# A state-space block with a binarised MLP on one core: scan tiles laid out in interleaved pairs, the norm's inverse root as a power on POOL, buffers in thirds

## The chip, the core and the metric

One of the cores of a Trainium2 chip runs the whole kernel. The metric is the device time in microseconds (us) of one execution; three executions of the kernel before took 3263.69, 3261.21 and 3260.56 us, median 3261.21.

The engines are called as the profile calls them: PE (TensorE, matmuls), PEld (its weight loads), DVE (VectorE), ACT (ScalarE), POOL (GpSimd) and SP (SyncE, which here only issues DMAs).

## The reference, cut to what matters

The input x is 8 images of 384 channels and 32 x 32 places; all data are float32. B = 8, C = 384, L = 1024.

```python
# norm over channels, twice (eps 1e-6, then 1e-5)
t = layernorm(ln_c(x)) * ln_w + ln_b                    # (b, L, 384)
xm, z = split(t @ in_proj_w.T)                          # 768 each
xc = silu(causal_conv_3_taps(xm) + conv_b)
dt, Bm, Cm = split(xc @ x_proj_w.T, [24, 40])           # 24, 16, 16
dt = softplus(dt @ dt_proj_w.T + dt_proj_b)             # (b, L, 768)
dA  = exp(dt[..., None] * A)                            # (b, L, 768, 16)
dBu = (dt * xc)[..., None] * Bm[:, :, None, :]
h_t = dA_t * h_(t-1) + dBu_t                            # scan over L
y = sum_n(h * Cm) + xc * D
t = (y * silu(z)) @ out_proj_w.T
x = x + gelu(t @ mlp_w1.T + mlp_b1) @ mlp_w2.T + mlp_b2
# the second layer, of which only the first 5 images get a part other than zero
q = quantise(ln_t(x) @ sign(W1 - mean).T + b1)          # per image: clip(a * 128 / (max|a| + eps))
x = x + quantise(gelu(q) @ sign(W2 - mean).T + b2)
```

The rows of W1 and W2 fall into 5 groups, each with a mean of its own.

## The kernel before, in words

The kernel is written as a list of operations which a planner in it, `Plan` (lines 163 to 349), puts into an order. Each `add` names an engine, a budget in us, the tiles it reads and writes, and a function that issues the instructions. `Plan.run` (line 221) goes through a simulated time: it takes the engine that can start first, chooses by lane and image (`rank`, line 256), issues the operation, and reckons its end from the budget. A DMA's end is reckoned at lines 332 to 334: 1.0 us after its issue, then its bytes at 395e3 per us on one shared line, then 0.9 us. The engines run what the planner issued in that fixed order, each its own queue. Where PE would be idle for over 0.7 us in the plan, lines 311 to 321 issue short matmuls without use, the tile `spare`. Buffers are rings of a fixed number (line 369), and a piece of work starts only when its ring has a free buffer.

For each image b, in halves of T = 512 places:

- `s1` (line 598), the front. `norm` (line 543) sums over channels with column-strip matmuls (`columns`, p_sum and p_var), spreads the mean over the partitions with a matmul (`spread`, p_mean), subtracts, squares, takes Sqrt on ACT and the reciprocal on DVE (lines 585 to 590), and spreads that (p_r). Then p_in and the convolution, Silu in place on the whole 128 x 3072 tile `xc`, p_dbc (dt's 24 rows, B and C), p_bc (line 698, which adds the two halves of B and C), six matmuls p_dt (line 722), Softplus, dt * xc on POOL (line 732), and the gate p_z with Silu. The results go to DRAM: xc, z, dt and dtx as whole tiles of 1.5 MB, B and C as rows.
- `s2` and `scan` (lines 748 and 761), the scan. A unit m holds four groups of 32 channels. For images 1 to 6 a tile is 128 x 1024: 32 channels times four of the 16 states, over all places. Images 0 and 7 are scanned in two halves with a tile of two groups by 512 places and a kept `state`. `rep` loads dt and dtx with every row repeated four times, `quad_rows` a row of B or C for each state. `scan_tile` (line 870) makes, for each tile: da = exp(dt * A) on ACT, into PSUM; u = dtx * B on POOL (line 886); the scan on DVE (line 890); the product with C on POOL (line 904) or on DVE (line 907), as `on_pool` (line 866) says. Then py (line 842) sums over the states with matmuls of 32 columns, four of which fill the array, and `zr` takes y * silu(z) to DRAM. Both inputs of POOL's products lie in SBUF; DVE's da lies in PSUM.
- `s3` (line 912): out_proj (p_out), the MLP's first matmuls (p_h), Gelu on two tiles of 128 x 3072, and the second ones (p_o, `mlp_out`, line 977).
- `ffn` (line 1092) for images 0 to 4: norm, p_y from the binarised W1, the maximum, then y1 again from DRAM in tiles of 1.5 MB, clip on POOL, Gelu, p_y from W2, the maximum, clip, addition. `binarise` (line 988) runs once: it sums W by matmuls with ones (p_sums, line 1018), takes the means and the signs.

The matmuls of most stages have line 494, ACT's functions line 510, and copies with a scale and a bias 523 to 532 (`affine`, which the planner may give to ACT, DVE or POOL).

Of the kernel before, what the change touches and what calls it, by code (L numbers as in the profile page):

```python
# [26 lines left out]
F32 = mybir.dt.float32  # L27
# [15 lines left out]
HK = KH // 2  # L43
T = 512
# [49 lines left out]

def c_pool(n):
    return 0.18 + n * 0.00214
# [33 lines left out]
class Piece:  # L130
# [8 lines left out]

    def __getitem__(self, part):  # L140
        return self, part

# [13 lines left out]
class Op:  # L156
    __slots__ = (
        "engine", "cost", "emit", "prio", "slack", "table", "size",
        "wants", "next", "ready", "tiles", "others", "settle",
# [3 lines left out]
class Plan:  # L163
# [12 lines left out]
    def add(self, engine, cost, emit, r=(), w=(), claim=(), table=None, size=0, others=None):  # L176
# [3 lines left out]
        op.size, op.prio = size, (*self.prio, len(self.ops))  # L180
# [40 lines left out]
    def run(self):  # L221
# [60 lines left out]
        while left:  # L282
# [49 lines left out]
            if e == "SP":  # L332
                dma_free = max(dma_free, end + 1.0) + op.size / 395e3
                end = dma_free + 0.9
# [17 lines left out]
class Layer:  # L352
    def __init__(self, ctx, tc, a, out):
# [9 lines left out]
        def ring(tag, bufs, where=sbuf):  # L363
# [7 lines left out]
            "front": ring("front", 2), "t_f": ring("t_f", 2), "w_f": ring("w_f", 3),  # L371
            "dbc": ring("dbc", 1), "halo": ring("halo", 2),

            "dt_r": ring("dt_r", 3), "dtx_r": ring("dtx_r", 3), "u": ring("u", 9),
# [4 lines left out]
            "yg": ring("yg", 1), "hid": ring("hid", 2), "t_b": ring("t_b", 1), "w_b": ring("w_b", 3),  # L379
            "w6": ring("w6", 2), "w6_n": ring("w6_n", 2), "res": ring("res", 2),  # L380

            "t_n": ring("t_n", 2), "small": ring("small", 7),

            "mm": ring("mm", 3, psum), "sq": ring("sq", 1),
            "rstd": ring("rstd", 2),
# [6 lines left out]
        for b in range(B):  # L392
            for name in ("dt", "dtx"):
                self.dram[name, b] = handed(f"{name}_d{b}", [DI, L])
# [24 lines left out]

    def constants(self):
        nc, a, const = self.nc, self.a, self.const
        small = const.tile([P, 3], F32, name="small")
        one, self.eps_m, self.eps_f = (small[:, i : i + 1] for i in range(3))
        for at, value in ((one, 1.0), (self.eps_m, E1 * E2), (self.eps_f, E_FFN)):
            nc.vector.memset(at, value)
# [8 lines left out]
        self.pick = const.tile([P, 2 * NS], F32, name="pick")  # L436
        nc.vector.tensor_add(self.pick, ident[:, DQ : 2 * DQ], ident[:, DP + DQ : DP + 2 * DQ])
        self.edge = const.tile([P, KD, 2], F32, name="edge")
# [23 lines left out]
    def load(self, to, view, src, r=(), size=0, cost=0.4):  # L462

        self.plan.add(
            "SP", cost, lambda: self.nc.sync.dma_start(view(to.real), src), r=r, w=[to],
            size=size,
        )

    def store(self, dst, frm, view, w, size, cost=0.4):
# [802 lines left out]
```

## Time and profile before

| | before |
|---|---|
| median of three executions | 3261.21 us |
| the profiled execution, and its span | 3262.23 us, 3260.4 us |
| mean granted clock of PE | 0.984 |
| DMA traffic | 748.73 MB in 367345 packets, 230 GB/s |

PE's busy time holds the pipelined matmuls with their modelled ends; each float32 matmul stands as two records, so that x1152 is 576 matmuls. A group's line gives: source line, engine, operation, output and inputs, shapes, count, busy us, mean ns of one record, and the idle time of that engine just before it with what ended it. The costliest that the change leaves alone are:

```profile
L494 PE MATMUL p_h<-t,w_b 128*128 128x512 f32 x1152 | 513.6, 600 | 10.9 <-DMA w_b<-in_mlp_w 9.9
L494 PE MATMUL p_o<-g,w 128*128 128x512 f32 x1152 | 506.7, 595 | 5.4 <-ACT g L510 2.9
L890 DVE TENSOR_TENSOR_SCAN da<-da,u 128x1024 f32<-128x1024 f32 (+1 forms) x416 | 840.5, 2020 | 111.6 <-POOL u L886 62.9
L890 DVE TENSOR_TENSOR_SCAN u<-da,u 128x1024 f32<-128x1024 f32 (+1 forms) x352 | 699.5, 2010 | 90.3 <-ACT da L510 63.0
```

The transfers that the change touches, with KB each and the median us from issue to landing:

```profile
dtx_r<-dtx_d SPq DMA_DIRECT2D x144, 512.0 KB, 5.8
dt_r<-dt_d SPq DMA_DIRECT2D x144, 512.0 KB, 6.0
w_b<-in_mlp_w SPq DMA_DIRECT2D x192, 192.0 KB, 2.9
...
w_f<-in_in_proj_w SPq DMA_DIRECT2D x168, 192.0 KB, 4.2
...
gf<-y_d SPq DMA_DIRECT2D x20, 1536.0 KB, 9.5
```

### The profile page before, as it was taken

To read this page: it belongs to the slowest core of one execution; us is meant where nothing else is said; L and a number is where in the kernel's file an instruction comes from. 1 tells how busy PE (TensorE), PEld (TensorE's weight loads), DVE (VectorE), ACT (ScalarE), POOL (GpSimd) and SP (SyncE) were. 2 spreads that over 40 slices of the span, in tenths; PEclk is the share of its full clock that TensorE was granted. 3 is DMA by queue.
4 is the path that set the end of the run, shared out by engine and by line. 5 is a ranking of instruction groups with operands and counts; after the bars stand their busy time and mean duration, and the time that the engine had idled before them with its cause. 6 is when DMAs were issued, how large, how long until landed. Compare 5 with 4: busy or idle time off the path is not lost.

```text
span 3260.4 us, 34027 instructions
## 1 busy us (share of the span) xinstructions
PE 3122.5 (96%) x11098; PEld 1317.7 (40%) x11098; DVE 2742.3 (84%) x2127; ACT 2024.3 (62%) x2246; POOL 2848.7 (87%) x1371
## 2 busy tenths in 40 slices
PE   8988999999999999999899999999999999999999
PEld 4333433444433434334334344343443534433334
DVE  4778899799978899888998878999788988789880
ACT  4778787656665576665656566755666565656551
POOL 1688899979999989999989999989999899999970
PEclk9998999999999999999999999999999999999999
DMA  6988778657796568675686667866677656766542
GB/s 218 305 282 276 249 250 294 221 183 234 259 322 197 184 230 291 229 238 197 208 298 211 237 211 246 295 225 226 220 275 250 207 185 205 249 187 207 167 141 76
DMA packets 367345, 748.73 MB, mean 230 GB/s; under 512 B 33856, under 2 KB 111168, under 8 KB 367168
## 3 DMA queue, kind: packets, MB, share of 16 engines
q1 hardware_dynamic: 366736, 746.46, 68.5%
q8 instruction: 89, 1.46, 0.2%
q14 instruction: 88, 0.72, 0.1%
q10 hardware_dynamic: 432, 0.09, 0.0%
HBM read 566.06 MB, written 180.36 MB: 229 GB/s over the span
## 4 chain that ended last, share of the span: by engine, by line
PE 74%; DMA 9%; DVE 6%; ACT 5%; issue 2%; POOL 2%; SPq 1%; ACTq 0%; DVEq 0%; POOLq 0%
PE p_y L494 17%; PE p_o L494 14%; PE p_h L494 13%; PE py L842 9%; PE p_out L494 6%; PE p_z L494 6%; PE p_in L494 5%; DVE da L890 2%; DMA w<-in_out_proj_w 2%; DMA w_f<-in_in_proj_w 2%; DVE u L890 1%; ACT L510 1%; DMA w_b<-in_mlp_w 1%; ACT da L510 1%; PE spare L412 1%
## 5 line engine op out<-in xcount | busy, mean ns | idle before, releaser
L886 POOL TENSOR_TENSOR u<-dtx_r,bc 128x1024 f32<-128x1024 f32 x768 | 1790.4, 2362 | 72.3 <-DMA dtx_r<-dtx_d 46.3
L510 ACT ACTIVATE da<-dt_r,a_neg 128x1024 f32<-128x1024 f32 (+1 forms) x960 | 902.7, 945 | 534.0 <-DVE u L907 331.1
L904 POOL TENSOR_TENSOR u<-u,bc 128x1024 f32<-128x1024 f32 x352 | 828.4, 2364 | 121.5 <-DVE u L890 115.5
L890 DVE TENSOR_TENSOR_SCAN da<-da,u 128x1024 f32<-128x1024 f32 (+1 forms) x416 | 840.5, 2020 | 111.6 <-POOL u L886 62.9
L890 DVE TENSOR_TENSOR_SCAN u<-da,u 128x1024 f32<-128x1024 f32 (+1 forms) x352 | 699.5, 2010 | 90.3 <-ACT da L510 63.0
L494 PE MATMUL p_h<-t,w_b 128*128 128x512 f32 x1152 | 513.6, 600 | 10.9 <-DMA w_b<-in_mlp_w 9.9
L907 DVE TENSOR_TENSOR u<-da,bc 128x1024 f32<-128x1024 f32 x416 | 507.9, 1221 | 10.5 <-ACT state L901 0.3
L494 PE MATMUL p_o<-g,w 128*128 128x512 f32 x1152 | 506.7, 595 | 5.4 <-ACT g L510 2.9
L842 PE MATMUL py<-u,fold 128*32 128x512 f32 x3072 | 376.6, 605 | 4.5 <-DVE u L907 4.5
L494 PEld LDWEIGHTS p_h<-t,w_b 128*128 128x128 f32 x1152 | 214.7, 190 | 298.1 <-issue 256.4
L494 PEld LDWEIGHTS p_o<-g,w 128*128 128x128 f32 x1152 | 215.9, 190 | 292.0 <-issue 277.3
L494 PE MATMUL p_y<-tn,w_b 128*128 128x512 f32 x720 | 324.9, 598 | 4.0 <-DVE tn L592 3.3
L494 PE MATMUL p_y<-gf,w_n 128*128 128x512 f32 x720 | 319.0, 599 | 6.7 <-DMA w_n<-bin_w 4.0
L510 ACT ACT_TABLE_LOAD x222 | 284.8, 1283 | 11.7 <-DVE xc L661 7.3
L494 PE MATMUL p_out<-yg,w 128*128 128x512 f32 x552 | 249.2, 604 | 8.9 <-DMA w<-in_out_proj_w 4.3
L494 PE MATMUL p_z<-t,w_f 128*128 128x512 f32 x504 | 232.5, 611 | 8.2 <-DMA w_f<-in_in_proj_w 6.2
L494 PE MATMUL p_in<-t,w_f 128*128 128x512 f32 x504 | 228.3, 602 | 10.8 <-DMA w_f<-in_in_proj_w 8.6
L494 PEld LDWEIGHTS p_y<-gf,w_n 128*128 128x128 f32 x720 | 135.1, 191 | 187.6 <-issue 172.4
L494 PEld LDWEIGHTS p_y<-tn,w_b 128*128 128x128 f32 x720 | 133.9, 190 | 183.9 <-issue 155.4
L842 PEld LDWEIGHTS py<-u,fold 128*32 128x32 f32 x3072 | 81.5, 110 | 261.1 <-issue 203.2
L525 ACT ACTIVATE g<-p_h,v_vecs 128x512 f32<-128x512 f32 x157 | 106.3, 681 | 120.9 <-PE p_h L494 120.7
L525 ACT ACTIVATE y<-p_y,v_vecs 128x512 f32<-128x512 f32 x138 | 94.1, 683 | 130.0 <-PE p_y L494 100.3
(112 smaller groups left out, 2700.3 us busy)
## 6 DMA issues: line engine op xcount, KB each, us to landing
dtx_r<-dtx_d SPq DMA_DIRECT2D x144, 512.0 KB, 5.8
dt_r<-dt_d SPq DMA_DIRECT2D x144, 512.0 KB, 6.0
w_b<-in_mlp_w SPq DMA_DIRECT2D x192, 192.0 KB, 2.9
w<-in_mlp_w SPq DMA_DIRECT2D x96, 384.0 KB, 3.6
w_f<-in_in_proj_w SPq DMA_DIRECT2D x168, 192.0 KB, 4.2
y_d<-y SPq DMA_DIRECT2D x120, 256.0 KB, 3.4
gf<-y_d SPq DMA_DIRECT2D x20, 1536.0 KB, 9.5
xc_d<-xc SPq DMA_DIRECT2D x16, 1536.0 KB, 7.3
```

Source lines behind the costliest of these rows:

```text
L412: self.plan.fill = lambda: self.nc.tensor.matmul(self.plan.spare.real[:, : 2 * P], self.ones, self.one.to_broadcast([P, 2 * P]), start=Tru ...
L494: self.nc.tensor.matmul(p.real, w.real[:, w0 + k, :], t.real[:, k0 + k, :], start=start and k == 0, stop=stop and k == n - 1,)
L510: lambda: self.nc.scalar.activation(out(), in_(), func, **{k: v() if callable(v) else v for k, v in kw.items()}),
L525: nc.scalar.activation(out(), in_(), AF.Identity, bias=bias, scale=scale)
L842: nc.tensor.matmul(py.real[p0 : p0 + DQ, :], self.fold, hc, start=False, stop=(q == NQUAD - 1), skip_group_check=True,)
L886: add("POOL", 2.36, lambda: nc.gpsimd.tensor_mul(u.real, dtx_r.real, spread(bq)), r=[dtx_r, bq], w=[u])
L890: add("DVE", (0.2 if half else 0.15) + n * 0.00209, lambda k=k, col=col: nc.vector.tensor_tensor_scan(to.real[:, k, :], da.real[:, k, :], ...
L904: add("POOL", 2.36, lambda: nc.gpsimd.tensor_mul(u.real, u.real, spread(cq)), r=[cq], w=[u])
L907: add("DVE", 1.21, lambda: nc.vector.tensor_mul(u.real, da.real, spread(cq)), r=[da, cq], w=[u])
```

## The change

1. **Interleaved pairs.** Two scan tiles lie in one buffer u of [128, wide, n, 2], the second tile's elements between those of the first. POOL multiplies both in one instruction, with B or C repeated for each pair. DVE's scan and product and the py matmuls read and write the pair's halves with a stride of two elements. The last quarter of the states writes into the dtx buffer itself. Channels are regrouped on the host to suit. `on_pool` gives POOL the C product of 9 in 16 tiles (before 11 in 24).
2. **Norm.** p_var is scaled and copied, turned by a matmul with columns of the identity (p_turned), and eps is added on DVE; POOL raises [128, 4] to the power -0.5. The Sqrt and the reciprocal go.
3. **Front.** p_bc becomes p_all, one matmul that adds the halves of B and C and copies dt's rows twice, to partitions 0 and 32; p_dt then runs in pairs on two strips of 32 rows. dt * xc writes interleaved.
4. **Thirds.** xc, z, dt, yg, the MLP's g and gf are tiles of [128, 2, 512], with the activations, the stores and loads on them in thirds or sixths. yg, z of image 1 and the MLP's pieces share one ring of nine; p_o runs in six parts of two matmuls.
5. **Binarise.** p_sums uses 32-column strips of the array; the groups are summed on DVE, and a small matmul (p_means) adds the lanes.
6. **Planner.** A transfer's end is reckoned with a landing time by kind, and budgets of issues are changed.

```diff
@@ planner, rings
+def c_pair(n):
+    return 0.19 + n * 0.00188
...
             if e == "SP":
-                dma_free = max(dma_free, end + 1.0) + op.size / 395e3
-                end = dma_free + 0.9
+                dma_free = max(dma_free, end + 0.5) + 0.05 + op.size / 360e3
+                end = dma_free + op.land
...
-            "front": ring("front", 2), "t_f": ring("t_f", 2), "w_f": ring("w_f", 3),
+            "front": ring("front", 7), "t_f": ring("t_f", 2), "w_f": ring("w_f", 3),
...
-            "dt_r": ring("dt_r", 3), "dtx_r": ring("dtx_r", 3), "u": ring("u", 9),
+            "dt_r": ring("dt_r", 3), "dtx_r": ring("dtx_r", 2), "u": ring("u", 3),
...
-            "yg": ring("yg", 1), "hid": ring("hid", 2), "t_b": ring("t_b", 1), "w_b": ring("w_b", 3),
-            "w6": ring("w6", 2), "w6_n": ring("w6_n", 2), "res": ring("res", 2),
-
-            "t_n": ring("t_n", 2), "small": ring("small", 7),
+            "hid": ring("hid", 9), "t_b": ring("t_b", 1), "w_b": ring("w_b", 3),
+            "w6": ring("w6", 2), "w6_n": ring("w6_n", 2), "res": ring("res", 4),
+
+            "t_n": ring("t_n", 2), "small": ring("small", 4),
...
-    def load(self, to, view, src, r=(), size=0, cost=0.4):
+    def load(self, to, view, src, r=(), size=0, cost=0.46, land=2.3):
...
-        self.load(w, lambda t: t, src, r=r, size=4 * P * k * P, cost=0.34)
+        self.load(w, lambda t: t, src, r=r, size=4 * P * k * P, cost=0.37, land=1.5)
@@ norm
-        rstd = self.piece("rstd", [P, TG], "rstd")
-        self.act(
-            lambda: rstd.real, lambda: p_var.real, AF.Sqrt, c_act(TG), r=[p_var], w=[rstd],
-            table="sqrt", bias=eps, scale=scale,
-        )
-        add("DVE", 0.93, lambda: nc.vector.reciprocal(rstd.real, rstd.real), w=[rstd])
-        p_r = spread(rstd, "p_r")
+        var = self.piece("rstd", [P, TG], "var")
+        self.affine(lambda: var.real, lambda: p_var.real, [p_var], [var], scale=scale, n=TG)
+        p_turned = self.piece("mm", [P, G], "p_turned")
+        add("PE", 0.5, lambda: nc.tensor.matmul(
+            p_turned.real, var.real, self.ident[:, ::DQ], start=True, stop=True
+        ), r=[var], w=[p_turned])
+        rstd = self.piece("root", [P, G], "rstd")
+        add("DVE", 0.1, lambda: nc.vector.tensor_scalar_add(rstd.real, p_turned.real, eps),
+            r=[p_turned], w=[rstd])
+        add("POOL", 0.8, lambda: nc.gpsimd.tensor_tensor(
+            rstd.real, rstd.real, self.power.to_broadcast([P, G]), ALU.pow
+        ), w=[rstd])
+        p_r = spread(rstd, "p_r", True)
@@ s1
+            p_all = self.piece("mm", [P, T], "p_all")
+            n_all = DP + 2 * NS
+            add("PE", MM, lambda dbc=dbc, p_all=p_all: nc.tensor.matmul(
+                p_all.real[:n_all, :], self.join, dbc.real, start=True, stop=True
+            ), r=[dbc], w=[p_all])
...
+                def two(k=k, pds=pds, dbc=dbc, ws=ws):
+                    for i in range(2):
+                        rows = slice(i * DQ, (i + 1) * DQ)
+                        nc.tensor.matmul(
+                            pds[i].real, ws[i].real[rows, (k + i) % KC, :], dbc.real[rows, :],
+                            start=True, stop=True,
+                        )
...
+                dtx = self.piece("sq", [P, T, 2], "dtx")
+                add("POOL", 2.35, lambda p=p, dtx=dtx, xc=xc, dt=dt: nc.gpsimd.tensor_mul(
+                    dtx.real.rearrange("p n i -> p i n"), xc.pieces[p].real, dt.pieces[p].real
+                ), r=[xc[2 * p], xc[2 * p + 1], dt[2 * p], dt[2 * p + 1]], w=[dtx])
@@ scan
+                u = dtxs if q == NQUAD - 1 else self.piece("u", [P, wide, n, 2], "u")
+                self.scan_pair(
+                    u, [[(k * G + g) * NQUAD + q for k, g in groups] for groups in tiles],
+                    n, dts, dtxs, b_q[q], c_q[q], state, half, self.on_pool(q, m),
+                )
...
-    def on_pool(self, i, q, m):
-
-        return q == 0 or (q == 2 and (i == 0 or m % 3))
+    def on_pool(self, q, m):
+
+        return q % 2 == 0 or (q == 1 and m % 4 == 0)
...
+        def product(t, x, row):
+            nc.gpsimd.tensor_mul(
+                u.real[:, x], t.real[:, x], row.real.unsqueeze(2).to_broadcast([P, n, 2])
+            )
+        for x in range(wide):
+            add("POOL", c_pair(2 * n), lambda x=x: product(dtxs, x, bq), r=[dtxs[x], bq],
+                w=parts[x])
...
+            def in_u(i, t=t):
+                return u.real[:, 0, :, t] if wide == 1 else u.real[:, t, :, i]
+
+            to = (lambda i: in_u(i)) if on_pool else (
+                lambda i, da=da: da.real[:, i, :])
...
+        if on_pool:
+            for x in range(wide):
+                add("POOL", c_pair(2 * n), lambda x=x: product(u, x, cq), r=[cq], w=parts[x])
@@ s3, binarise
+            g = self.split("hid", KH, "g")
...
+            for k in range(0, HK, PER):
+                need = [g[i * HK + k + j] for j in range(PER)]
+                self.matmuls(po, w, g, i * HK + k, PER, i + k == 0, i * HK + k + PER == KH, need,
+                             claim, k)
...
+                    g = k % lanes
                     nc.tensor.matmul(
-                        pm.real, self.ones, w.real[:, k - ks.start, :],
-                        start=(k == 0), stop=(k == kt - 1),
+                        pm.real[g * DQ : (g + 1) * DQ, :], self.ones[:, :DQ],
+                        w.real[:, k - ks.start, :], start=(k < lanes), stop=(k >= kt - lanes),
                     )
```

## The prediction

> **What bounds the kernel now.** I read the totals and the slices first, then the chain of work that ended last, the groups with shapes kept apart, the waits of the matmul engine, and the stretches. The totals, three rows of the slices, and the chain's two lines:
>
> ```profile
> PE 3122.5 (96%) x11098; PEld 1317.7 (40%) x11098; DVE 2742.3 (84%) x2127; ACT 2024.3 (62%) x2246; POOL 2848.7 (87%) x1371
> PE   8988999999999999999899999999999999999999
> POOL 1688899979999989999989999989999899999970
> PEclk9998999999999999999999999999999999999999
> ...
> PE 74%; DMA 9%; DVE 6%; ACT 5%; issue 2%; POOL 2%; SPq 1%; ACTq 0%; DVEq 0%; POOLq 0%
> ```
>
> TensorE (PE) is busy for 3122.5 of 3260.4 us from the second slice to the last and makes 74% of the chain. It is the bound, with 138 us idle. POOL, at 87%, is full in most slices after the first five: a second bound close behind. DMA is 9% of the chain. The groups that the change touches:
>
> ```profile
> L886 POOL TENSOR_TENSOR u<-dtx_r,bc 128x1024 f32<-128x1024 f32 x768 | 1790.4, 2362 | 72.3 <-DMA dtx_r<-dtx_d 46.3 <-PE py L842 21.6 <-issue 2.4
> L904 POOL TENSOR_TENSOR u<-u,bc 128x1024 f32<-128x1024 f32 x352 | 828.4, 2364 | 121.5 <-DVE u L890 115.5 <-PE p_in L494 1.0 <-POOL u L886 0.6
> L907 DVE TENSOR_TENSOR u<-da,bc 128x1024 f32<-128x1024 f32 x416 | 507.9, 1221 | 10.5 <-ACT state L901 0.3
> L842 PE MATMUL py<-u,fold 128*32 128x512 f32 x3072 | 376.6, 605 | 4.5 <-DVE u L907 4.5
> L510 ACT ACT_TABLE_LOAD x222 | 284.8, 1283 | 11.7 <-DVE xc L661 7.3 <-PE p_var L552 0.6
> L722 PE MATMUL p_dt<-dbc,w_f 128*128 128x512 f32 x168 | 81.9, 620 | 9.5 <-ACT dt L525 6.0 <-ACT rows L523 3.4
> L412 PE MATMUL spare<-small 128*128 128x256 f32 x314 | 80.0, 396 | 0.1
> L690 PE MATMUL p_dbc<-xc,w_f 128*64 128x512 f32 x168 | 41.0, 625 | 0.8 <-ACT sums L1025 0.6
> ```
>
> Each matmul stands as two records. POOL's two products are 2619 of its 2849 us. The waits of PE's matmuls, longest in total first:
>
> ```profile
> PE p_var L552 <- ACT sq L510: 10.9, 2, 5.7
> PE p_r L567 <- DVE rstd L590: 10.5, 6, 3.7
> PE p_h L494 <- DMA w_b<-in_mlp_w: 9.9, 6, 2.8
> PE p_in L494 <- DMA w_f<-in_in_proj_w: 8.6, 6, 6.4
> ```
>
> The rows of that answer that end on a DMA sum to 56 us; those of the norm (p_sum, p_mean, p_var, p_r) to about 34 us. The chain in order of time prices a break between matmul shapes:
>
> ```profile
> 2092.11 10.30 PE p_out L494 x24
> 2104.26 5.35 PE p_y L494 x12
> ```
>
> Twelve matmuls in one run take 10.30 us, six alone 5.35: 2 x 5.35 - 10.30 = 0.4, so 0.2 us per break; the time between the two is a py group, whose matmuls use another shape of the array.
>
> **What the Trainium skill says.** GPSIMD Engine Reference, section 3.1: a two-input elementwise operation is held by its two reads sharing one port; 4497 ns for 2048 fp32. The trace gives 2362 ns for 1024, so two make 4.72 us; one of twice the size saves a fixed part only, if the page holds. TensorE: Matmul & The Clock Gate, Part 3: matmuls on different 32-row strips run at once (3.07 times for four). The trace has no row strips, but column strips do: the 1536 py matmuls take 376.6 us, 0.98 us for four. SBUF — State Buffer, Door 1: two fp32 hits in a 16-byte line keep full rate, which a stride of two elements has; no run of before has such a stride.
>
> **Part by part.** Counts are those of the two built programs.
>
> *PE.* p_dt: 96 matmuls take 93.3 us (81.9 and 11.4 for the other weight ring). After, 48 pairs on two row strips. A pair that runs at once costs what a p_dbc pair of column strips does: 46.6 us (41.0 and 5.6) over 48 pairs is 0.97, and 0.2 for the break that each pair now is: 56 us. That is -37. If the strips don't overlap, 93 + 48 x 0.2 = 103, +10; I take -37. p_sums: 21 full matmuls, 18.7 us, become six groups of three or four column strips at about 0.9 with a break each, and two small ones: 7.7, so -11. p_bc, 6.7 us, becomes 16 full p_all at 0.97, 15.5: +9. p_turned adds 26 small matmuls; p_max, also small, takes 4.6 us for ten: 26 x 0.46 = +12. Changes of the array's shape in the built order rise from 498 to 569; 48 are in the p_dt term, the other 23 cost +5. Sum: -37 - 11 + 9 + 12 + 5 = -22 us. py reads with a stride of two: from 0 (the page) to twice its 377 us; I take 0. Below nothing isn't possible, as the matmuls stay the same in number. Fillers (spare) rise from 157 to 192 at 0.51 us, +18; they stand only where the plan leaves PE idle, so I count them with idle time, 138 + 80 = 218 us now.
>
> *POOL.* The 768 + 352 products of 1024 become 450 of 2048 and 304 of 1024 with the row operand repeated for each two elements (pair share on POOL for C: from 46% to 56%). Price p of the 2048 one: upper end 4.72 (twice the row), 4.50 by the page; lower end if the repeated row is fetched once per pair, 1.5 reads in place of 2: 0.2 + 2048 x 1.6 ns = 3.5. The 1.6 is three quarters of the row's slope, (2362 - 180) / 1024 = 2.13 ns, with 180 ns from the shortest POOL copies (L898, 187). I take the middle of 3.5 and 4.5, 4.0. The rest of POOL is 230 us; less 119 for L732, plus 48 pair products for it at 2.36 (113), 26 powers at an unknown price (0.2, as other tiny POOL operations, to 3 us; I take 0.8: 21), more pieces of clip and edge (11): 256. Halves cost p/2 + 0.09. Total 602p + 27 + 256: 2691 at 4.0, against 2849. Off the path as long as PE's is longer.
>
> *DVE.* 332 products for 416: -84 x 1.22 = -103; 26 reciprocals of 0.94 go, -24; small additions +9. 2742 becomes about 2624. Strided output: 0 by the page to 252 x 1.2 = 300 us at half rate; I take 0.
>
> *ACT.* 222 table loads become 178: -56. A hundred big activations (2.77) become 300 thirds at about 1.11: +55. No change, and at 62% it is covered. If that cover were gone, each front would wait 0.6 us longer for its third piece: 16 x 3 x 0.6 = 29 us.
>
> *Norm.* Sqrt, its two table switches (2 x 1.28) and the reciprocal (0.94) go; one copy, p_turned, an addition and the power come, with two more hand-overs. The power stands in POOL's queue, in order, behind a product of 4 us (2 on average), and p_r, the multiplication after it, and the projection wait for it; behind the power stand the next products. Only 6 of 26 norms showed a p_r wait (10.5 us). Bounds: -10 to 26 x 4 = +104 if PE had nothing else; I take 0 as other lanes' matmuls are ready.
>
> *Queues and transfers.* SP issues 2253 DMAs for 2089: +164 x 0.5 (0.42 to 0.60 in the chain) = 82 us, on a queue that issues for about 1050 of 3260. Loads of dtx fall from 240 to 120 with the same bytes; pieces of xc, z, dt, gf and yg triple. SP's order matters at the head only, where a unit has 14 issues for 12, +1 us. The plan's price of a transfer was 1.9 us + bytes / 395 per ns: 2.4 us for 192 KB, where w_f took 4.2 and w_b 2.9; 3.2 for dt_r's 512 KB, which took 6.0; 5.9 for yg's 1.5 MB, which took 9.0. Now it adds a landing time by kind, so that loads stand earlier. Of the 56 us of PE's DMA waits I expect a third back: -20 (bounds 0 to -56). Rings of thirds let stores start after a third of the work; what is late next there is PE itself.
>
> Profiled execution: 3262.2 - 22 - 20 = 3220 us. It lies 1 us above the median, so 3220 stands for both.
>
> **Rivals.**
>
> *POOL becomes the bound (slower).* The stretches say:
>
> ```profile
> 650.00:3100.00 2450.00, 2371.42 (x8354) 996.41 (x8353) 2154.14 (x1579) 1492.50 (x1584) 2289.43 (x1058) 0.99 0.68 229
> ```
>
> The fifth busy column is POOL: 2289 of 2450 us, 93%, and 80% of its whole work. At p = 4.5, the page's price, its total is 2992, 80.4% of that is 2404, and at 97% full the stretch lasts 2479: +29, 3291 us. It decides from 97% x 2450 / 0.804 = 2957 us of total, p = 4.44. For it: the page's price, and that halves with the row repeated over a whole tile cost no less than the others. Against: an operand that repeats at once can spare a fetch. 13%. A stride that slows py by over 42 of 377 us, 11%, has the same sign: at 20%, 3295 us. 5%.
>
> *Row strips run one after the other.* p_dt +10 for -37: 3267 us, no change or a bit slower. 8%. For it: no row strip in the trace; against: the page.
>
> *The waits go too.* All of PE's DMA waits and the norm's go, 56 + 34: 3262 - 22 - 90 = 3150. For it: POOL and DVE lose 120 to 160 us each and pieces of a third start their followers sooner. Against: the built order has more fillers, not fewer. 17%.
>
> **Numbers.** Forecast 57%, own range 3195 to 3250. Range for all: 3150 to 3290; below it half of the last rival (8%), above it half of POOL's and most of the stride's (11%). About 0.2%, 6.5 us, is what a measurement tells from no change. Faster: 53 of the forecast's 57, 17, and a little of the rivals' edges: 0.72. Same: 4 of the forecast and part of the strips' rival, 0.07. Slower: 13, 5 and the rest, 0.21.
>
> **What would show it.** Right: p_dt pairs near 1.2 us and some 55 us in all; the 2048 product near 4.0 us, POOL near 2690; py still near 0.98 per four; DVE near 2620; PE's busy time near 3120 with the fillers; PE's DMA waits near 35 us. Wrong: a pair product above 4.44 with POOL's slices all 9, longer py records, or p_r waits on the power that sum to more than 20 us.

## The result, and the profile after

The changed kernel takes 3256.44 us (median of 20 executions, 3248.79 to 3262.76), the kernel before on the same chip 3264.39 us (20 executions, 3252.38 to 3273.85): a ratio of 0.9974 [0.9964, 0.9983], 8 us faster (the brackets hold the 95% interval, here and below). The forecast was 42 us faster.

The page of the changed kernel, its totals, the same rows of the slices, and the chain by engine:

```profile
PE 3137.5 (96%) x11128; PEld 1310.6 (40%) x11128; DVE 2641.6 (81%) x2076; ACT 1981.5 (61%) x2369; POOL 2750.3 (85%) x1051
PE   9888999999989999999999999999999999999999
POOL 1878879988998878999899899899889999999780
PEclk9898999999999999999999999999999999999999
...
PE 75%; DMA 7%; POOL 6%; DVE 5%; ACT 3%; issue 2%; SPq 1%; POOLq 0%; DVEq 0%; ACTq 0%
```

The three figures that the forecast built on have hardly moved. PE is busy 15 us longer in a span 8 us shorter (3252.4 for 3260.4); its slices are as full as they were, and the chain is still PE's, 75% for 74%, with POOL at 6% where it had 2%. POOL lost 98 us of work and DVE 101, and the end of the kernel didn't come earlier by anything like that. The long stretch, in the same columns as before:

```profile
650.00:3100.00 2450.00, 2397.16 (x8378) 998.61 (x8377) 2078.61 (x1528) 1468.78 (x1675) 2199.20 (x746) 0.99 0.69 230
```

The fifth busy column, POOL, fell from 2289 to 2199 us in this stretch, and PE's rose from 2371 to 2397. But not all of PE's time is of use. These are the groups with shapes kept apart:

```profile
L925 POOL TENSOR_TENSOR u<-dtx_r,bc 128x2048 f32<-128x2048 f32 x216 | 882.3, 4095 | 151.6 <-PE py L890 86.7 <-issue 59.3 <-DMA w<-in_out_proj_w 3.6
L890 PE MATMUL py<-u,fold 128*32 128x512 f32 x2304 | 303.6, 626 | 3.2 <-POOL u L925 1.6 <-DVE u L972 1.6
L890 PE MATMUL py<-dtx_r,fold 128*32 128x512 f32 x768 | 104.2, 612 | 0.0
L434 PE MATMUL spare<-small 128*128 128x256 f32 x384 | 100.4, 397 | 4.3 <-ACT z L552 1.9 <-DVE z L559 1.6 <-DVE t L631 0.4
L766 PE MATMUL p_dt<-dbc,w_f 32*128 32x512 f32 x168 | 55.3, 692 | 6.5 <-DVE rstd L625 2.3 <-DVE q L1173 1.2 <-DVE tn L611 0.9
L627 POOL TENSOR_TENSOR rstd<-rstd,small 128x4 f32<-128x4 f32 x26 | 26.4, 1016 | 18.8 <-DVE rstd L625 17.3 <-DVE mean L1129 1.4
```

Reading down: the product of a pair takes 4.095 us (two of before: 4.72). The records of py took 605 ns before; now they take 626 where the pair lies in u, and 612 where it lies in dtx_r. The fillers (spare) rose from 80 to 100 us. p_dt, 93 us before, is here 55 and 9 more in the other weight ring. The power takes 1.016 us.

A busy PE record overlaps the next one, so I also summed PE's timeline from each start to the next:

| PE, us | before | after | difference | forecast |
|---|---|---|---|---|
| p_dt | 90.7 | 62.6 | -28 | -37 |
| p_sums, with p_means | 17.8 | 6.7 | -11 | -11 |
| p_bc, then p_all | 5.8 | 15.7 | +10 | +9 |
| p_turned | 0 | 7.2 | +7 | +12 |
| py | 362.5 | 376.5 | +14 | 0 |
| all of use (busy time of the page, less spare) | 3045.0 | 3040.1 | -5 | -22 |
| spare | 77.5 | 97.4 | +20 | +18 |
| idle (span less the page's busy time) | 137.9 | 114.9 | -23 | |
| idle and spare together | 215.4 | 212.3 | -3 | -20 |

The forecast's -22 has +5 more, for changes of the array's shape; they have no row of their own, as what they took lies in the other rows. The last four lines are the whole account: -5 of use and -3 of waiting make the 8 us. The mean granted clock is nearly the same in both, 0.984 and 0.983. And the waits of PE's matmuls:

```profile
PE p_h L523 <- DMA w_b<-in_mlp_w: 11.5, 7, 2.7
PE p_z L523 <- DMA w_f<-in_in_proj_w: 11.4, 3, 6.6
PE p_r L599 <- POOL rstd L627: 6.2, 6, 1.6
```

All rows of this answer that end on a DMA sum to 39.4 us, 55.7 before: -16, about what was forecast. The idle time fell with them, and the fillers grew by as much.

### The profile page after: what moved, and what is told of

Read it like the earlier page. It is cut to its first block, busy times and chain, and to the rows that moved or that the text cites. A ratio compares the mean times of both kernels' runs of the same rounds, so it can differ in the third digit from the quotient of the medians.

```text
span 3252.4 us, 34130 instructions
## 1 busy us (share of the span) xinstructions
PE 3137.5 (96%) x11128; PEld 1310.6 (40%) x11128; DVE 2641.6 (81%) x2076; ACT 1981.5 (61%) x2369; POOL 2750.3 (85%) x1051
## 4 chain that ended last, share of the span: by engine, by line
PE 75%; DMA 7%; POOL 6%; DVE 5%; ACT 3%; issue 2%; SPq 1%; POOLq 0%; DVEq 0%; ACTq 0%
PE p_y L523 16%; PE p_h L523 14%; PE p_o L523 13%; PE py L890 9%; PE p_out L523 7%; PE p_z L523 6%; PE p_in L523 5%; POOL u L925 4%; DVE u L950 2%; DVE da L950 1%; DMA w_f<-in_in_proj_w 1%; PE spare L434 1%; DMA w_b<-in_mlp_w 1%; PE p_dt L766 1%; ACT da L539 1%
## 5 line engine op out<-in xcount | busy, mean ns | idle before, releaser
L925 POOL TENSOR_TENSOR u<-dtx_r,bc 128x2048 f32<-128x2048 f32 (+1 forms) x360 | 1187.0, 3311 | 167.5 <-PE py L890 97.9
L925 POOL TENSOR_TENSOR u<-u,bc 128x2048 f32<-128x2048 f32 (+1 forms) x274 | 901.3, 3294 | 91.2 <-DVE u L950 87.5
L950 DVE TENSOR_TENSOR_SCAN u<-da,u 128x1024 f32<-128x1024 f32 (+1 forms) x436 | 867.8, 2006 | 106.0 <-POOL u L925 58.0
L523 PE MATMUL p_h<-t,w_b 128*128 128x512 f32 x1152 | 514.0, 600 | 11.6 <-DMA w_b<-in_mlp_w 11.5
L950 DVE TENSOR_TENSOR_SCAN da<-da,dtx_r 128x1024 f32<-128x1024 f32 (+1 forms) x192 | 388.0, 2021 | 80.6 <-POOL dtx_r L925 57.9
L925 POOL TENSOR_TENSOR dtx_r<-dtx_r,bc 128x2048 f32<-128x2048 f32 (+1 forms) x120 | 396.9, 3313 | 1.2
L950 DVE TENSOR_TENSOR_SCAN da<-da,u 128x1024 f32<-128x1024 f32 (+1 forms) x140 | 286.3, 2045 | 30.8 <-ACT da L539 17.1
L890 PE MATMUL py<-u,fold 128*32 128x512 f32 x2304 | 303.6, 626 | 3.2 <-POOL u L925 1.6
L970 DVE TENSOR_TENSOR dtx_r<-da,bc 128x1024 f32<-128x1024 f32 x144 | 176.3, 1224 | 3.6
```

The costliest lines, as they stand in the source:

```text
L523: self.nc.tensor.matmul(p.real, w.real[:, w0 + k, :], t.at(k0 + k), start=start and k == 0, stop=stop and k == n - 1,)
L890: nc.tensor.matmul(py.real[g * DQ : (g + 1) * DQ, :], self.fold, hc, start=False, stop=(q == NQUAD - 1), skip_group_check=True,)
L925: nc.gpsimd.tensor_mul(u.real[:, x], t.real[:, x], row.real.unsqueeze(2).to_broadcast([P, n, 2]))
L950: da=da, in_u=in_u: nc.vector.tensor_tensor_scan(to(i), da.real[:, i, :], in_u(i), state.real[:, col : col + 1] if half else 0.0, ALU.mult ...
L970: nc.vector.tensor_mul(u.real[:, 0, :, t], da.real[:, 0, :], cq.real)
```

## The experiments

My theory after the result: PE's work and its waits are no longer terms that can be subtracted one for one. The planner's order is fixed, and in it PE, POOL, DVE and the loads take turns in setting the pace; what is taken from one is mostly waited for at the next. Beside it stood four narrower ones: the stride in py eats the gain; the longer products on POOL hold the rest back; the fillers cost what the waits gave; and the order that the planner found was a poor one, or the one before a lucky one. Kernels were timed with the kernel before on the same chip, whose medians lay at 3264.56 to 3267.31 us. Each stands on 4 to 22 executions. Below, what a kernel takes more or less than after is the difference of the two ratios to before, times 3264 us. I split PE's time in three: its work of use (all matmuls but the fillers), the fillers, and its idle time.

### In the order of after: one cost at a time

**The stride.** py reads four contiguous quarters of the pair's buffer in place of every second element, so it sums other elements than the reference's; all else, the order too, is as in after.

```diff
-                        parts = [u.real[:, 0, h, i] for i in both for h in HALVES] if ...
+                        flat = u.real.rearrange("p x n i -> p (x n i)")
+                        parts = [flat[:, k * T : (k + 1) * T] for k in range(G)]
```

> The changed kernel in the same order; the py matmuls read four contiguous quarters of each pair buffer instead of every second element, so their sums mix the wrong elements: this leaves out the right pairing, nothing of the work. Theory (the stride of two costs py its 14 us): py falls from 376 to about 362 us of PE time, its records from 612 to 592 ns, and the time falls by 8 to 14 us. Rival (py is longer because the order breaks it up or it waits): py stays near 376 and the time within 3 us.

3244.68 us, 0.9939 [0.9918, 0.9960] of before: 11 us less than after, give or take 8 by the two intervals. The py groups of this kernel, shapes kept apart:

```profile
L890 PE MATMUL py<-u,fold 128*32 128x512 f32 x2304 | 292.5, 609 | 2.8 <-POOL u L925 1.5 <-DVE u L972 1.3
L890 PE MATMUL py<-dtx_r,fold 128*32 128x512 f32 x768 | 101.8, 602 | 0.0
```

The records fell from 626 and 612 ns to 609 and 602, and py's time from start to start from 376.5 to 363.0 us, that of before. The stride costs 14 us of PE and about 11 of the span: the term that I had put at 0.

**Less PE work.** Of every three matmuls of p_h the middle one is left out, so a third of its sum is missing; the order is the same.

```diff
-            for k in range(n):
+            for k in (0, n - 1) if p.name == "p_h" else range(n):
```

> The changed kernel in the same order, with one of the three matmuls of each p_h left out (the middle third of the channels does not enter the MLP): 192 matmuls, 169 us less for PE. Theory (PE is the bound nearly everywhere): 120 us or more faster. Rival (the scan's chain of POOL and DVE sets the pace and PE only fills in): 50 us faster or less, and PE's idle time grows by over 100 us.

3211.50 us, 0.9831 [0.9806, 0.9856]: 47 us less than after, for 137 us less of p_h from start to start. If PE alone set the time, all of it would show. Its waits:

```profile
PE p_h L523 <- DMA w_b<-in_mlp_w: 56.6, 26, 6.5
PE p_o L523 <- DMA w<-in_mlp_w: 13.4, 9, 4.7
```

In after p_h waited 11.5 us for its weights, 7 times; with a third of its matmuls gone it waits 56.6, 26 times, and all DMA waits of PE grow from 39 to 92 us. PE's idle time grew by 85 us in all: 53 of them are these waits on DMA, 29 are waits on ACT and DVE. The rest of PE's work took 10 us longer, at a mean granted clock of 0.973 for 0.983. So behind PE stand, right there, the loads of weights first, and ACT and DVE next. Of the two expectations the rival has the time, but neither its idle time (over 100 us) nor its reason: it is the loads that hold PE up, more than the scan. The cut is in a stage that streams them, so this says how close the loads are in that stage, not in all.

**Less POOL work.** The products with C on POOL cover half of the columns; the other half of u stays without it.

```diff
-                u.real[:, x], t.real[:, x], row.real.unsqueeze(2).to_broadcast([P, n, 2])
+                u.real[:, x, :k], t.real[:, x, :k], row.real[:, :k].unsqueeze(2).to_broadcast([P, k, 2])
```

> The changed kernel in the same order, POOL's product with C over half the columns only (the other half of those states is summed without C): about 440 us less for POOL. Theory (PE is the bound): at most 20 us faster. Rival (POOL and the scan set the pace): 80 us faster or more.

3246.48 us, 0.9944 [0.9924, 0.9963]: 10 us less than after, for 425 us less on POOL (2750 to 2326). POOL is not the bound, so the rival that made it one falls for this kernel; the pair product, at 4.095 us, had already come in below the 4.44 from which that rival would have held.

**Both cuts together:**

> Kernel after in its own order, with both cuts that were made singly before: a third of the p_h matmuls is left out, and the products with C on POOL cover only half of the columns. Alone they gave -45 and -10 us. If each engine were bound by its own work, the two would add: -55, 3202. If PE and POOL take turns as the bound in one fixed order, together they give clearly more than the sum: 3150 to 3190.

3189.38 us, 0.9773 [0.9750, 0.9797]: 66 us less than after, for 47 and 10 alone. That is 9 more than the sum of 57, which the intervals (8 us each way for this run alone) don't tell from it, at the very edge of the range that I gave for taking turns. PE and POOL in turn explain little: with both cuts PE still had 177 us of idle time and 97 of fillers, and 81 us of DMA waits. The theory in its strong form isn't shown. The weaker one is: PE's time can't be subtracted one for one, and in p_h it is mostly the loads that stand right behind it.

**No fillers.** The call that issues them is gone.

```diff
-                    self.fill()
```

> The changed kernel in the same order without the 192 fillers, 97 us of PE time. Theory (fillers stand in real idle time and only take its name): within 6 us, PE busy near 3040 and idle near 210. Rival one (fillers hold up matmuls that were ready): 15 to 60 us faster. Rival two (they keep PE's clock up): slower, with a lower granted clock.

3254.74 us, 0.9974 [0.9964, 0.9983], the same ratio as after. Idle and spare together fell from 212 to 172 us, but the mean granted clock fell too, from 0.983 to 0.973, and PE's work of use took 3087 us in place of 3040. The fillers neither cost nor gain here: the 40 us that they take they give back in the clock. So their increase is not where the gain went.

### In a new order: one part undone

These kernels are planned anew, so each has an order of its own. How far that alone moves the time is asked further down.

**The old norm** (Sqrt on ACT and the reciprocal on DVE, as in the diff of the change, backwards):

> The changed kernel with the norm of before (Sqrt on ACT, reciprocal on DVE), planned anew. Theory (PE's useful time and the waits it cannot avoid decide): PE loses p_turned's 7 us, table loads rise again by some 40, p_r waits about 4 us more; within 6 us of the changed kernel's 3256. Rival (the Sqrt's table switches were what the change gained): 10 us slower or more.

3281.06 us, 1.0048 [1.0031, 1.0065]: 24 us more than after. PE's work of use is the same (3043 us for 3040); what grew is idle time and fillers, 239 us for 212. Whether the table switches of the Sqrt made that or the new order did, this run can't tell.

**p_dt as whole matmuls**, without the row strips:

```diff
-                            pds[i].real, ws[i].real[rows, (k + i) % KC, :], dbc.real[rows, :],
+                            pds[i].real, ws[i].real[:, (k + i) % KC, :], dbc.real,
...
-                add("PE", MM + 0.2, two, ...
+                add("PE", 2 * MM, two, ...
```

> The changed kernel with p_dt as whole matmuls over 128 rows, one after the other (the weights' second copy is zero), planned anew. Theory (PE's useful time counts one for one when the plan knows it): p_dt 63 to about 91 us, 20 to 30 us slower. Rival (PE's useful time counts in part only, as with the p_h third left out: 45 of 169): 4 to 10 us slower.

3298.78 us, 1.0107 [1.0088, 1.0126]: 43 us more. p_dt took 92.3 us again, 30 more than after, so the row strips run side by side: two of them in 1.30 us for 1.92, a gain of 1.47 (the Trainium skill, TensorE: Matmul & The Clock Gate, Part 3, has 3.07 for four). Idle time and fillers rose as well, by 24 us (236 for 212), while the rest of PE's work took 13 us less, at a mean granted clock of 0.989 for 0.983.

**The old reckoning of transfers' ends** in the planner; the instructions stay:

```diff
-                dma_free = max(dma_free, end + 0.5) + 0.05 + op.size / 360e3
-                end = dma_free + op.land
+                dma_free = max(dma_free, end + 1.0) + op.size / 395e3
+                end = dma_free + 0.9
```

> The changed kernel planned with the transfer ends of before (1.0 us, 395e3 bytes per us, 0.9 us). Theory (foreseen waits become fillers and unforeseen ones idle time, and the sum of both stays at about 206 us): fewer fillers, more idle, within 6 us. Rival (the prices by kind place loads earlier and save real waits): 10 us slower or more, PE's waits on DMA up from 39 us to 55 or more.

3318.15 us, 1.0161 [1.0141, 1.0181]: 61 us more. Its span and mean granted clock, and PE's waits in it:

```profile
core 0: 3318.1 us, clock 0.973
...
PE p_z L523 <- DMA w_f<-in_in_proj_w: 22.8, 10, 4.5
PE p_h L523 <- DMA w_b<-in_mlp_w: 14.9, 11, 2.9
PE p_o L523 <- DMA w<-in_mlp_w: 9.1, 7, 3.8
```

All of them on DMA sum to 83.7 us for 39.4: loads are planned to land earlier than they do, and PE meets them. But idle time and fillers together grew by 24 us only (236 for 212). The other 42 us of the span (3318 for 3252) are PE's work of use, which took 3082 us for 3040 at a granted clock of 0.973 for 0.983.

**The new reckoning in the kernel before**, with a landing time of 1.5 us for weights and 2.0 for the rest:

```diff
-                dma_free = max(dma_free, end + 1.0) + op.size / 395e3
-                end = dma_free + 0.9
+                dma_free = max(dma_free, end + 0.5) + 0.05 + op.size / 360e3
+                end = dma_free + (1.5 if op.cost == 0.34 else 2.0)
```

> The kernel before, planned with the transfer ends of the change (0.5 us, 0.05 us and 360e3 bytes per us, landing 1.5 us for weights, 2.0 for the rest). Theory (an unforeseen wait costs more than a foreseen one, as taking the prices away cost the changed kernel 62 us): 15 to 60 us faster than before. Rival (the prices matter to the changed kernel only, since its buffers are tighter): within 10 us of before or slower.

3251.92 us, 0.9964 [0.9949, 0.9978], 12 us less than before: this one edit gives the kernel before as much as the whole change gave, or a little more (the intervals overlap). Its span and clock, its fillers, and two of its waits:

```profile
core 0: 3247.8 us, clock 0.993
...
L412 PE MATMUL spare<-small 128*128 128x256 f32 x456 | 114.6, 393 | 2.1 <-ACT rstd L510 1.4 <-ACT y L525 0.4 <-ACT g L525 0.2
...
PE p_in L494 <- DMA w_f<-in_in_proj_w: 5.7, 3, 3.8
PE p_h L494 <- DMA w_b<-in_mlp_w: 5.4, 7, 1.8
```

p_h's wait for its weights is 5.4 us for 9.9 and p_in's 5.7 for 8.6; all DMA waits of PE sum to 20.7 us for 55.7. Yet idle time and fillers together did not fall: the idle time lost 27 us, the fillers gained 34, and the sum is 222 us for 215. All of the gain is in PE's work of use, the same matmuls in 3026 us for 3045, at a granted clock of 0.993 for 0.984. More on this below.

**No pairs.** After with separate tiles of 128 x 1024, the old split of the products with C, seven buffers u and three of dtx_r in the place of three pairs and two:

```diff
-            "dt_r": ring("dt_r", 3), "dtx_r": ring("dtx_r", 2), "u": ring("u", 3),
+            "dt_r": ring("dt_r", 3), "dtx_r": ring("dtx_r", 3), "u": ring("u", 7),
...
-                u = dtxs if q == NQUAD - 1 else self.piece("u", [P, wide, n, 2], "u")
-                self.scan_pair(
...
+                us = []
+                for i, groups in enumerate(tiles):
+                    self.scan_tile(
```

> The changed kernel without the pairs: two separate tiles of 1024 as before, their own dtx loads, POOL's products one by one at 2.36 us and its old share of the C products, seven buffers for u and three for dtx; the rest as in the change. Theory (the pairs relieve POOL and DVE, which are not the bound, and cost PE 14 us): between 20 us faster and 10 us slower than 3256, POOL's busy time up by about 100. Rival (the pairs are what pays): 20 us slower or more.

3320.50 us, 1.0162 [1.0148, 1.0175]: 61 us more than after. The totals of its page:

```profile
PE 3185.4 (96%) x11408; PEld 1364.9 (41%) x11408; DVE 2730.5 (82%) x2148; ACT 1989.4 (60%) x2394; POOL 2883.7 (87%) x1403
```

POOL has 133 us more work than in after, and PE's idle time and fillers are 293 us for 212 (135 idle, 158 spare), while its py takes 365.5. PE's work of use takes 13 us less (3027 for 3040), so all that was lost is idle time and fillers. So in the company of the rest of the change the pairs are worth much more than the stride costs. How much of it is the shorter products and how much that two tiles need less room, the run doesn't part: the kernel before has nine buffers u and this one seven, as the other rings have grown.

### How much is the order alone

The three parts undone singly and the reckoning cost 24 + 43 + 61 + 61 = 189 us, where the whole gave 8. So I asked what a new order does with no part changed. The planner's price of a matmul, MM, is 0.86 us; moved by 0.005 it leaves PE's matmuls of use as they are in number (10744 records in the changed kernel, 10784 in the one before, in each of the three orders). It changes what is issued when, and with that how many fillers there are and which engine makes some of the small copies.

```diff
-MM = 0.86
+MM = 0.855
```

> The changed kernel with the plan's price of a matmul 0.855 for 0.86: the same work in another order. It shows how much of a difference is the luck of an order. Theory: within 6 us of 3256. Rival: 10 us or more to either side, and then single parts of this size cannot be told apart by planning anew.

> The changed kernel with 0.865: a third order of the same work, beside the 14 us slower one with 0.855. Theory (luck of the order of some 10 to 20 us): 5 to 25 us slower than 3256. Rival: within 5 us of it, and 0.855 was an outlier.

> The kernel before, planned with 0.855 for 0.86 as the price of a matmul: the same work in another order. Theory (both kernels stand on an order that came out well, and any new order costs 10 us or more): 10 to 30 us slower than before. Rival (the old order is no luck): within 6 us.

> Kernel before, with only the planner's price of a matmul set to 0.865 us in place of its own: same instructions, another order. If the order before was a lucky one, this one is slower by 5 to 30 us (3270 to 3295), as the other re-ordering of it was by 27. If that one was an accident, within 5 us of before.

After took 1.0005 [0.9994, 1.0016] at 0.855 and 0.9972 [0.9962, 0.9983] at 0.865; before took 1.0079 [1.0065, 1.0092] and 1.0076 [1.0055, 1.0097]. The order is worth up to 11 us in the changed kernel and 25 to 26 in the one before, and the kernel before stood on the best of its three. In its two other orders PE's work of use took 3053 and 3048 us for 3045; the rest is idle time and fillers, 244 and 239 us for 215.

**Prices from the trace.** If the planner errs because its prices are off, those that the trace of after shows should help: the pair product, the power, p_dt, p_turned, p_all, thirds, clip.

```diff
-    return 0.19 + n * 0.00188
+    return 0.181 + n * 0.001911
...
-        add("POOL", 0.8, lambda: nc.gpsimd.tensor_tensor(
+        add("POOL", 1.02, lambda: nc.gpsimd.tensor_tensor(
...
-                add("PE", MM + 0.2, two, ...
+                add("PE", 1.3, two, ...
```

> Kernel after, with the planner's prices set to what the trace of after shows: pair products 0.181 + 1.911 ns per element, the power 1.02, a p_dt pair 1.3, p_turned 0.28, p_all 1.0, Gelu and Silu thirds 1.05, clip 0.28 + 0.9 ns per element. If wrong prices cost the change its gain, 3225 to 3245. If orders only scatter, anything from 3250 to 3275.

3267.99 us, 1.0008 [0.9997, 1.0020]: 11 us more than after. Prices closer to the trace gave one more order, and not a better one.

**The reckoning in second orders.** At MM = 0.855 the kernel before with the new reckoning, and at 0.865 the changed kernel with the old one:

> Kernel before with the new reckoning of transfers' ends, and the price of a matmul at 0.855: a pair to the re-ordering of before at that price, which took 1.0079 of before. If the reckoning is worth something in any order, clearly below that, 0.99 to 1.003 (3235 to 3275). If its effect in the first order was an accident of order, 1.005 to 1.012.

> Kernel after with the old reckoning of transfers' ends, and the price of a matmul at 0.865: a pair to after at that price, which took 0.997 of before. If the +62 us of the first order without the new reckoning is the reckoning's, this again takes 1.010 to 1.020 of before (3297 to 3330). If it was an accident of order, 0.997 to 1.005.

3262.89 us, 0.9992 [0.9983, 1.0001], and 3336.68 us, 1.0215 [1.0189, 1.0240]. With these the reckoning has two pairs of orders in each kernel:

| ratio to before | MM | old reckoning | new reckoning | the reckoning's worth |
|---|---|---|---|---|
| kernel before | 0.86 | 1 | 0.9964 | 12 us |
| | 0.855 | 1.0079 | 0.9992 | 28 us |
| | 0.865 | 1.0076 | | |
| changed kernel | 0.86 | 1.0161 | 0.9974 | 61 us |
| | 0.865 | 1.0215 | 0.9972 | 79 us |
| | 0.855 | | 1.0005 | |
| | trace's prices | | 1.0008 | |

Read across, the reckoning pays in every pair: 20 us in the kernel before (mean of two), 70 in the changed one. Read down, the rest of the change, all of its new instructions, buffers and budgets of issues, is worth this: under the old reckoning the mean goes from 1.0052 (three orders) to 1.0188 (two), 44 us slower; under the new one from 0.9978 (two) to 0.9990 (four), 4 us slower, between 7 faster and 14 slower by the extremes. **The gain is the reckoning's; the rest, taken together, gives nothing that these runs can show.**

How the reckoning pays is another matter. These are the profiled executions of the same four pairs, old reckoning and then new:

| | MM | PE's work of use, us | idle and fillers, us | PE's waits on DMA, us | mean granted clock |
|---|---|---|---|---|---|
| kernel before | 0.86 | 3045, 3026 | 215, 222 | 56, 21 | 0.984, 0.993 |
| | 0.855 | 3053, 3024 | 244, 238 | 51, 37 | 0.980, 0.991 |
| changed kernel | 0.86 | 3082, 3040 | 236, 212 | 84, 39 | 0.973, 0.983 |
| | 0.865 | 3050, 3038 | 285, 213 | 88, 57 | 0.981, 0.983 |

PE waits less for DMAs in every pair, but in the kernel before hardly any of that left the sum of idle time and fillers: there the gain is PE's work of use, which ran at a higher granted clock. In the changed kernel some of it is that (42 us of 66 in the first pair, 12 of 84 in the second), and the rest is a smaller sum of idle time and fillers. The work of use times the clock is nearly the same in all eight kernels, 2986 to 3005 us, so the work got shorter about as the clock rose. This is not the chance of one execution: over all executions of the kernel before, the clock is 0.988 to 0.993 with the new reckoning, in both orders, and 0.980 to 0.986 with the old one. Why it rises isn't shown. The fillers may have a part: without them the changed kernel had the lower clock, and in three of the four pairs the new reckoning brings more of them. But no run takes them out of the kernel before with the new reckoning.

**A version with less stride.** Where DVE makes the product with C (7 of 16 pairs), it waits for both scans and writes the tiles one behind the other, so that py reads them contiguously. The rest is as in after, with an order of its own.

```diff
-                        nc.vector.tensor_mul(u.real[:, 0, :, t], da.real[:, 0, :], cq.real)
+                        nc.vector.tensor_mul(
+                            flat[:, 0, t * n : (t + 1) * n], da.real[:, 0, :], cq.real)
...
-                add("DVE", 1.21, by_dve, r=[da, cq], w=[u[t]])
+                late.append((by_dve, [da, cq], [u[0], u[1]] if wide == 1 else [u[t]]))
+        for go, r, w in late:
+            add("DVE", 1.21, go, r=r, w=w)
```

> Kernel after, but where DVE makes the product with C (7 of 16 pairs), it waits for both scans of the pair and writes the two tiles one after the other into the buffer, so that py reads those contiguously. The stride's cost in py falls by 7/16 of 14 us, 6 us: 3250 if only that counts. If the later products or the new order cost more than they save: 3255 to 3280.

3251.70 us, 0.9955 [0.9944, 0.9966]: 6 us less than after, the size that the stride would give, and the lowest of all kernels that leave nothing of the work or the pairing out, though its interval touches after's and an order can give as much. Its py groups:

```profile
L894 PE MATMUL py<-u,fold 128*32 128x512 f32 x2304 | 301.5, 623 | 2.0 <-POOL u L929 2.0
L894 PE MATMUL py<-dtx_r,fold 128*32 128x512 f32 x768 | 103.2, 596 | 3.0 <-DVE dtx_r L979 2.8
```

All pairs in dtx_r are contiguous now, and their records fall from 612 to 596 ns; a quarter of those in u are, 626 to 623. But py from start to start fell by 2 us only (374.3 for 376.5) in the profiled execution, which had a granted clock of 0.979, so that the 6 us are the stride's isn't shown.

## Why the prediction was wrong, point by point

**What held.** p, taken as 4.0, was 4.095, and the halves 2.135 for 2.09; 602 x 0.095 is 57 us, the gap between 2691 and the 2750 measured. DVE came to 2642 for 2624. p_dt on two strips did overlap (1.30 us a pair for 1.17), p_sums and p_all were right to 1 us. The norm's hand-overs didn't cost: p_r waits 6.2 us for the power, 10.5 for DVE before. PE's DMA waits fell to 39.4 us for a forecast of 36. "Off the path as long as PE's is longer" was right of POOL.

**The steps that failed.** Two, in the prediction's own sum, 3262.2 - 22 - 20.

1. *"py reads with a stride of two: ... I take 0", and with it the -22.* PE's work of use fell by 5. py's 14 us are the largest part of the miss, p_dt's pairs 9 more. The Trainium skill (SBUF — State Buffer, Door 1) says that two hits in a line of 16 bytes keep the full bandwidth; a stride of two fp32 elements has two hits, and py's matmuls took 376.5 us for 363.0 in the same order. The measurement decides: about 4%. I had the other end of the bound, twice 377, and a rival that began at 11%; a few per cent, in between, had no place in the sum.
2. *"Of the 56 us of PE's DMA waits I expect a third back: -20."* 16 of them came back, nearly what I forecast, and idle time and fillers together fell by 3. A shorter wait for a DMA did not make the span shorter by as much: in an order planned anew, other waits or fillers stand where those had been. The kernel before with the new reckoning shows it alone: 35 us of these waits went, and idle time and fillers grew by 6. I had counted fillers with idle time, which was right, but then subtracted a wait from the span without asking whether that sum would fall.

**What stood behind both.** I made the sum against one execution of one order and called it the kernel. The two other orders of the kernel before are 25 us slower; its mean is 1.0052, and after's is 0.9990. From mean to mean the change gives 0.62%, 20 us for the measured 8; so 12 of the 34 us of the miss lie in the orders, above all the good one that the kernel before happened to have. Of the 20, the reckoning alone makes as many in the kernel before. That is the size I had given to it, but by luck: in the kernel before it came as shorter work of PE at a higher clock, a term that my sum doesn't have, and not as a shorter wait. And the -22 for PE's work came to +4: the stride's 11 are a part of these 26; p_dt's 9 on PE may be another; the rest isn't shown.

**The rivals.** POOL as the bound: no, by its price and by the run with half of the C products. Row strips one after the other: no, as p_dt whole took 92 us for 63. All waits go: they didn't; 39 us of waits on DMA stayed.

**What stays open.** Undoing the pairs, the norm or p_dt costs 24 to 61 us each in the company of the rest, more than the 12 us by which after's orders differ, and yet the rest as a whole gives nothing. (Each was undone in one order only.) So something in it costs about as much as these give, or they are worth much only beside one another. The stride is 11 us of it. The thirds, the ring of nine and the smaller scan rings weren't taken out by themselves. One wait speaks for the rings, that of POOL's first products:

```profile
POOL u L925 <- PE py L890: 97.9, 46, 10.6
```

It was 21.6 us before: with three pairs in the ring, POOL waits for py to free one. The run with half of the C products says that a POOL which comes earlier gains 10 us, so this wait is no proof: that the smaller rings cost something is argued, not shown.

## What to carry to other kernels

Where a planner fixes the order, plan both kernels two or three times with a price moved by half a per cent before one says what a part is worth: here that alone moved one kernel by 25 us, three times what the change gave. Busy time taken from the fullest engine need not come back as time: of 137 us cut from PE's p_h, 47 came back, since loads stood right behind. A wait taken away need not come back either: look at idle time and fillers together, at the work of use, and at the granted clock beside them. And a later landing time for transfers in the plan was worth more here than all of the new instructions, at the cost of a few lines.

## What the runs showed of the hardware

- Matmuls whose moving operand (the data that streams through the array) has a stride of two fp32 elements took 626 and 612 ns a record, for 609 and 602 with the same order and contiguous operands: 14 us of 376. On DVE the same stride cost next to nothing: a scan of 1024 elements that reads and writes it took 2.283 us, for 2.278 before.
- A product on POOL whose second operand repeats each element twice takes 2.135 us for 1024 elements, where a plain one takes 2.362; 4.095 for 2048. The Trainium skill, GPSIMD Engine Reference, section 3.1, has 4.497 for a two-input addition of 2048; no plain product of 2048 was run here.
- A power of four elements in each of 128 partitions took 1.016 us on POOL, five times a small copy (0.190).
- Without the fillers the granted clock was 0.973 in place of 0.983, and PE's work of use took 47 us longer: short matmuls without use paid for themselves here, and no more.
- PE's work of use followed the mean granted clock: in the four pairs of the reckoning it took 3024 to 3082 us at clocks between 0.993 and 0.973, and the product of the two stayed within 2986 to 3005.
